# Queries, keys and values of a four-layer graph network from seven block products

## The chip, the cores and the metric

The kernel runs on one core of a Trainium2 chip. The metric is device time in microseconds of one execution. The five engines of the core work side by side: TensorE (PE, with its weight loads shown as PEld), VectorE (DVE), ScalarE (ACT), GpSimd (POOL) and SyncE (SP), which issues the DMA transfers. They wait for one another only through semaphores.

## The reference

128 graphs of 64 nodes with 256 features pass through four layers; before each, the features are normalised and clipped at zero, and each layer's result is added to them.

```python
# layers 0 and 1: attention with 8 heads of 32, masked by (or biased with the log of) the adjacency
q, k, v = h @ Wq, h @ Wk, h @ Wv                 # layer 0 with biases
attn = softmax(q @ k.T / sqrt(32) + mask)        # per head, over the 64 nodes of a graph
x = x + (attn @ v) @ Wo + bo
# layer 2: five steps of a gated unit over the graph
m = h @ weight[l]; agg = A.T @ m; h = gru(agg, h)
# layer 3: a gate between two products
x = x + elu(gate * (adj @ (h @ theta) * norm) * norm + (1 - gate) * (h @ W_h))
```

Everything is float32. The kernel takes 8 graphs at a time as a group: 512 tokens, four pairs of 128. There are 16 groups, and a group has two halves of 256 tokens.

## The kernel before

The kernel doesn't issue its instructions in the order in which they are written. Each operation is put into a plan with the engine, an assumed cost in ns, what it reads and writes, and a place in a strand; at the end the plan plays the five engines against each other, picks the next operation by its key among those that are ready, and so fixes the order of instructions on every engine. Parts of three groups are interleaved in this way: the attention of one, the gated unit of the one before, layer 3 of the one before that.

```python
def mm(n, count=1):                       # assumed cost of a float32 product of n columns
    return count * 2 * (n / 1.2 + 2.5)
INTO, OUT, BESIDE, ALONE = 110, 260, 0.3, 0.1   # into and out of small tiles; preferences in the choice
...
if found:                                 # in Plan.run: the choice of the next operation
    first = min(at for at, _ in found) + 15
    alone = ALONE if sum(t[1].small and t[0] <= first + 100 for t in found) < 2 else 0.0
    pick = min((t for t in found if t[0] <= first), key=lambda t: t[1].key + (
        (-BESIDE if small else alone) if t[1].small else 0.0))
```

The attention of one half. Weights of q, k, v stay in SBUF; `hT` holds the normalised features, transposed, in two chunks of 128 features.

```python
def attend(layer, xt, half, bias, bias_at, name):
    ...
    def dense(ps, wt, dst):
        for c in range(2):
            for kc in range(2):
                pe(mm(256), lambda c=c, kc=kc: nc.tensor.matmul(
                    ps[:, c * HALF : (c + 1) * HALF], wt[:, kc, c * P : (c + 1) * P], hT[:, kc, :],
                    start=kc == 0, stop=kc == 1), [wt, hT], [ps], holds=[dst])

    pq = bank(f"q_{name}")                       # one of 4 PSUM banks with tag "a"
    dense(pq, w["q"], qT)
    ...                                          # VectorE: q out of PSUM (+ bias in layer 0) into qT
    pk = bank(f"k_{name}")
    dense(pk, w["k"], k_exp)
    ...                                          # ScalarE: k out of PSUM, spread over two masked copies
    if waiting:
        ...
        def both():
            weigh_last()                         # of the half before: attn @ v, 32 products in 64x32 tiles
            scores()                             # of this half: q @ k.T, 16 products in 64x64 tiles
        pe(1440, both, [*reads, qT, k_exp], [*po_last, *pss], holds=[oT_last, *es], small=True)
        finish_last()
    else:
        pe(870, scores, [qT, k_exp], pss, holds=es, small=True)
    pv = bank(f"v_{name}")
    for gp in range(2):
        for kc in range(2):
            pe(mm(256), ...)                     # v
    sca(act(512), ...)                           # ScalarE: v out of PSUM
    ...                                          # softmax on DVE, ACT and POOL; four transposes
```

Elsewhere the kernel already forms 2x2 block products with seven in place of eight: in the gated unit (256 columns) and in layer 3 (384 columns), where two banks take turns and each product adds to what an earlier one left:

```python
def seven_products(hT, F, name):                 # layer 3
    T = new("hTT", [P, 4, P], 1, f"hTT_{name}")
    ...                                          # VectorE: 4 differences of blocks of hT
    product(1, pb, True)
    product(2, pc, True)
    total(pc, keep(pb, "l1"), 0, 0)              # keep: ScalarE evicts; total: VectorE adds
    product(5, pc, True)
    p5 = keep(pc, "l5")
    product(6, pb)
    u = keep(pb, "lu")
    product(3, pc)
    total(pc, u, 0, 1)
    product(7, pb)
    total(pb, p5, 1, 1)
    product(4, pb)
    ...
F = [new("F", [P, 3, D], 3, f"F_{g}_{2 * half + i}") for i in range(2)]      # 3 buffers
```

Of the kernel before, what the change touches and what calls it, by code (L numbers as in the profile page):

```python
# [46 lines left out]
INTO, OUT, BESIDE, ALONE = 110, 260, 0.3, 0.1  # L47
AHEAD = 1.7
# [4 lines left out]
FRONT_LAST = 0.1  # L53
FRONT_SPAN = 1.1
BACK = -0.1
BACK_LAST = 0.6
BACK_SPAN = 0.6
STEP = -0.2
# [8 lines left out]
FUSE = -1.05  # L67
# [3 lines left out]
def mm(n, count=1):  # L71
    return count * 2 * (n / 1.2 + 2.5)
# [45 lines left out]
class Op:  # L118
    __slots__ = ("eng", "cost", "lat", "fn", "key", "left", "users", "ready", "vals", "port", "small")


class Plan:
# [15 lines left out]
    def add(self, eng, cost, fn, reads=(), writes=(), lat=None, early=0.0, holds=(), port=False, small=False):  # L138

        op = Op()  # L140
        op.eng, op.cost, op.fn, op.users, op.ready = eng, cost, fn, [], 0.0
        op.lat = AFTER[eng] if lat is None else lat
        op.port, op.small = port, small
        op.key = self.at - early
        if eng == "PE":
            self.at += cost
        deps, vals = set(), []
        items = [(False, r) for r in reads] + [(True, w) for w in writes]
        items = [(wr, it if isinstance(it, tuple) else (it, None)) for wr, it in items]
        for wr, (v, part) in items:  # L150
            if v not in vals:
                vals.append(v)
            for table in (v.writers, v.readers) if wr else (v.writers,):
                for k, ops in table.items():
                    if part is None or k is None or k == part:
                        deps.update(ops)
        for wr, (v, part) in items:
            if wr:
                if part is None:
                    v.writers, v.readers = {}, {}  # L160
                v.writers[part], v.readers[part] = [op], []
            else:
                v.readers.setdefault(part, []).append(op)
        for v in holds:
            vals.append(v)
            for ops in v.readers.values():
                deps.update(ops)
        deps.discard(op)
        op.left = len(deps)
        for d in deps:  # L170
            d.users.append(op)
        op.vals = vals
        for v in vals:
            if not v.left and v.slots.queue is not None:
                v.slots.queue.append(v)
            v.left += 1
        self.ops.append(op)
# [6 lines left out]

    def run(self):
# [5 lines left out]
        ready, small = {e: [] for e in AFTER}, False  # L191
# [6 lines left out]
        for _ in range(len(self.ops)):  # L198
# [3 lines left out]
            for eng, ops in ready.items():  # L202
# [16 lines left out]
                if found:  # L219
                    first = min(at for at, _ in found) + 15  # L220
                    alone = ALONE if sum(t[1].small and t[0] <= first + 100 for t in found) < 2 else 0.0
                    pick = min((t for t in found if t[0] <= first), key=lambda t: t[1].key + (
                        (-BESIDE if small else alone) if t[1].small else 0.0))
                    if best is None or pick[0] < best[0]:
                        best = pick
# [9 lines left out]
            if op.eng == "PE":  # L235
                end += (INTO if op.small else OUT) if op.small != small else 0
                small = op.small
# [17 lines left out]
def gnn_stack_kernel(ctx: ExitStack, tc: tile.TileContext, a: dict, out: bass.AP):  # L255
# [18 lines left out]
    def new(tag, shape, n, name=None):  # L274
        if tag not in tags:
            home = psum if tag in ("a", "g") else dram if tag == "gates" else work
            tags[tag] = Slots(home, tag, n, tag in ("g", "ht", "agg", "Ta", "Th", "gv", "qT", "kexp", "v"))
# [8 lines left out]
    def pe(cost, fn, reads, writes, early=0.0, holds=(), small=False):  # L286
        plan.add("PE", cost, fn, reads, writes, early=early, holds=holds, small=small)
# [65 lines left out]
    with plan.strand(-3.0, 0.1):  # L353
# [31 lines left out]
        attn = [[{n: load_w(f"L0_gnn_W{n}", D) for n in "qk"}]]  # L385
# [11 lines left out]
        attn[0][0]["v"] = load_w("L0_gnn_Wv", D)  # L397
# [6 lines left out]
        attn[0][0]["o"] = load_w("L0_gnn_Wo", D)  # L404
        attn[0].append(load_row("L0_gnn_bo"))
# [3 lines left out]
        attn.append([{n: load_w(f"L1_gnn_W{n}", D) for n in "qkvo"}, load_row("L1_gnn_bo")])  # L409
# [22 lines left out]
    with plan.strand(-0.9, 0.1):  # L432

        w, bo = attn[0]
        bvb = new("aT", [P, 4, P], 2, "bvb")
        pbo = bank("bvo")
        for c in range(2):
            vec(200, lambda c=c: nc.vector.tensor_copy(
                bvb[:, c, :], cols[:, 16 + c : 17 + c].to_broadcast([P, P])), [cols], [(bvb, c)])
            pe(mm(256), lambda c=c, w=w: nc.tensor.matmul(  # L440
                pbo[:, :D], bvb[:, c, :], w["o"][:, c, :], start=c == 0, stop=c == 1),
                [(bvb, c), w["o"]], [pbo])
# [34 lines left out]
    def transposed(dst, dst_at, src, src_at, name, on_act, writes, relu=False, early=0.0,  # L477
# [12 lines left out]
        pe(437, turn, [*(reads or [src]), ident], [ps], early, [dst])  # L490
# [37 lines left out]


    waiting = []  # L530

    def attend(layer, xt, half, bias, bias_at, name):

        w, bo = attn[layer]
        biased = layer == 0
        pp = 2 * half
        hT = normed(xt, half, name, True)
        k_exp = new("kexp", [P, 2, 2, HALF], 1, f"kexp_{name}")
        qT = new("qT", [P, 2, HALF], 1, f"qT_{name}")

        def dense(ps, wt, dst):
            for c in range(2):
                for kc in range(2):
                    pe(mm(256), lambda c=c, kc=kc: nc.tensor.matmul(  # L544
                        ps[:, c * HALF : (c + 1) * HALF], wt[:, kc, c * P : (c + 1) * P], hT[:, kc, :],
                        start=kc == 0, stop=kc == 1), [wt, hT], [ps], holds=[dst])

        pq = bank(f"q_{name}")
        dense(pq, w["q"], qT)
        if biased:  # L550
            for c in range(2):
                vec(dve(256, 1), lambda c=c: nc.vector.tensor_scalar(
                    qT[:, c, :], pq[:, c * HALF : (c + 1) * HALF], cols[:, c : c + 1], None, op0=ALU.add),
                    [pq, cols], [(qT, c)])
        else:
            vec(dve(512), lambda: nc.vector.tensor_copy(
                qT.tile, pq.tile.rearrange("p (c t) -> p c t", c=2)), [pq], [qT])
        v = new("v", [P, 2, D], 2, f"v_{name}")
        pk = bank(f"k_{name}")
        dense(pk, w["k"], k_exp)  # L560

        for par in range(2):
            if biased:
                for c in range(2):
                    sca(act(256, 2), lambda c=c, par=par: nc.scalar.activation(
                        k_exp[:, c, par, :], pk[:, c * HALF : (c + 1) * HALF], AF.Identity,
                        bias=few[:, k_bias + 2 * c + par : k_bias + 2 * c + par + 1],
                        scale=few[:, parity + par : parity + par + 1]),
                        [pk, (few, 2), (few, 3 + c)], [(k_exp, (par, c))])
            else:  # L570
                sca(act(512, 1), lambda par=par: nc.scalar.activation(
                    k_exp[:, :, par, :], pk.tile.rearrange("p (c t) -> p c t", c=2), AF.Copy,
                    scale=few[:, parity + par : parity + par + 1]), [pk, (few, 2)], [(k_exp, (par, 0)), (k_exp, (par, 1))])
# [3 lines left out]
        def scores():  # L577
            for i in range(2):
                for c in range(2):
                    for gp in range(2):  # L580
                        for rh in range(2):
# [4 lines left out]
                                             qT[s, c, t0 : t0 + NODES], k_exp[s, c, :, t0 : t0 + NODES],  # L586
# [3 lines left out]
        if waiting:  # L590
            _, weigh_last, reads, po_last, oT_last, finish_last = waiting.pop()

            def both():
                weigh_last()
                scores()

            pe(1440, both, [*reads, qT, k_exp], [*po_last, *pss], holds=[oT_last, *es], small=True)
            finish_last()
        else:
            pe(870, scores, [qT, k_exp], pss, holds=es, small=True)  # L600

        pv = bank(f"v_{name}")
        for gp in range(2):
            for kc in range(2):
                pe(mm(256), lambda gp=gp, kc=kc: nc.tensor.matmul(  # L605
                    pv[:, gp * D : (gp + 1) * D], hT[:, kc, gp * P : (gp + 1) * P],
                    w["v"][:, kc, :], start=kc == 0, stop=kc == 1),
                    [w["v"], hT], [pv], holds=[v])
        sca(act(512), lambda: nc.scalar.activation(
            v.tile, pv.tile.rearrange("p (g f) -> p g f", g=2), AF.Copy), [pv], [v])  # L610
# [6 lines left out]
        for i in range(2):  # L617
# [25 lines left out]
            pe(437, turn, [e, ident], [pa], holds=[aT])  # L643
# [21 lines left out]
        def finish():  # L665
# [4 lines left out]
            for i in range(2):  # L670
                for c in range(2):
                    pe(mm(256), lambda i=i, c=c: nc.tensor.matmul(  # L672
                        py[:, i * D : (i + 1) * D], oT[:, i, c, :], w["o"][:, c, :],
                        start=c == 0, stop=c == 1), [(oT, i), w["o"]], [py])
# [6 lines left out]
    def flush(xt):  # L681
# [4 lines left out]
        pe(470, weigh, reads, po, holds=[oT], small=True)  # L686
# [16 lines left out]
    def fuse_weights(l):  # L703
# [11 lines left out]
        pe(437, turn, [gw[l], ident], [ps], holds=[wT, gv])  # L715
# [27 lines left out]
    def gru(h, ht, A, name):  # L743
# [19 lines left out]
        for l in range(LAYERS):  # L763
# [65 lines left out]
            pe(930, total, [ht, A], banks, holds=[agg], small=True)  # L829
# [120 lines left out]
    def front(g):  # L950
# [10 lines left out]
        for layer in range(2):  # L961
# [3 lines left out]
            for half in range(2):  # L965
# [3 lines left out]
                attend(layer, xt, half, bias, bias_at, f"{g}_{layer}_{half}")  # L969
# [23 lines left out]
        pe(437, turn, [blk, ident], [ps], holds=[adjT])  # L993
# [85 lines left out]
    def back_half(g, xt, h, adjT, norm, half):  # L1079
# [9 lines left out]
        pe(437, turn, [(h, (0, half)), (h, (1, half)), ident], [ps])  # L1089
# [8 lines left out]
        F = [new("F", [P, 3, D], 3, f"F_{g}_{2 * half + i}") for i in range(2)]  # L1098
# [40 lines left out]
    with plan.strand(FIRST, FIRST_SPAN):  # L1139
        for g in ORDER:  # L1140
            next(parts[g])
        for _ in parts[0]:
            pass
    for l in range(LAYERS):
# [68 lines left out]
```

## Time and profile before

| | |
|---|---|
| time, median of 3 runs | 2570.04 us (2569.54 to 2570.05) |
| span in the profile | 2566.7 us |
| granted TensorE clock | 0.998 |
| DMA traffic | 145.54 MB, mean 57 GB/s |
| q and k products | x512 instructions each, 386 and 382 ns mean |
| v products | x512 instructions, 381 ns mean |
| scores (s), weighing (o) | x2048 and x4096 instructions |
| aggregation (agg) | x5120 instructions |
| exp of the scores (ACT) | x128, 629 ns |

How to read it: a page gives for each engine its busy time; a group of instructions is named by the line of the kernel, the engine, the operation and what it writes and reads ("q<-hT,w_L_gnn_Wq"). The mean duration of one matmul is longer than the time it takes up in a stream, since matmuls overlap; the distance between the starts of two in a row is what a stream pays. "128*128" is the part of the array that a matmul uses, "128x256" its moving operand. Each float32 product stands in the trace as two weight loads and two matmuls.

### The profile page before, as it was taken

The numbers are of one execution on the slowest core, as the hardware profiler recorded it, in microseconds if no ns is written. First come the engines' busy times: TensorE is split into PE (matmuls) and PEld (weight loads), VectorE is DVE, ScalarE is ACT, GpSimd is POOL, SyncE is SP. The second block draws the span as 40 slices with busy tenths as digits, with TensorE's granted clock in tenths as the row PEclk, the third lists the DMA queues.
The fourth block names the chain that finished last, engine by engine and source line by source line (L and its number), as shares of the span: only waits on it lengthen the run. The fifth ranks groups of instructions, "written<-read, shape, count | busy, mean of one in ns | idle before, by whom it ended". The sixth has DMA issues, their size and how long they took to land.

```text
span 2566.7 us, 54470 instructions
## 1 busy us (share of the span) xinstructions
PE 2534.6 (99%) x22445; PEld 2129.0 (83%) x22445; DVE 1947.9 (76%) x4137; ACT 1308.8 (51%) x2452; POOL 870.4 (34%) x890
## 2 busy tenths in 40 slices
PE   8999999999999999999999999999999999999997
PEld 6788888888888888888888888888888888888885
DVE  6776677877777787787877878777777877777767
ACT  4445555555545555555554555555455455545543
POOL 5533332423233242432423324232332424323221
PEclk9999999999999999999999999999999999999999
DMA  5311111111111111211111111111111112011110
GB/s 156 119 64 56 58 44 61 44 48 61 49 57 44 48 61 48 76 35 59 43 67 57 44 65 44 48 57 48 57 44 48 57 48 77 24 48 70 61 57 17
DMA packets 44203, 145.54 MB, mean 57 GB/s; under 512 B 11106, under 2 KB 32820, under 8 KB 33076
## 3 DMA queue, kind: packets, MB, share of 16 engines
q1 hardware_dynamic: 43840, 142.03, 15.7%
q8 instruction: 177, 2.90, 0.5%
q14 instruction: 70, 0.57, 0.1%
q10 hardware_dynamic: 116, 0.04, 0.0%
HBM read 126.79 MB, written 15.27 MB: 55 GB/s over the span
## 4 chain that ended last, share of the span: by engine, by line
PE 96%; DVE 3%; ACT 0%; DMA 0%; issue 0%; POOL 0%; SPq 0%; DVEq 0%; POOLq 0%
PE gb L785 22%; PE gc L785 16%; PE nb L785 11%; PE nc L785 8%; PE q L544 4%; PE v L605 4%; PE k L544 4%; PE y L672 4%; PE agg L825 3%; PE l3b L1050 3%; PE s L585 3%; PE aT L640 2%; PE l3c L1050 2%; PE hT L488 2%; PE lnT L488 2%; PE o L659 2%
## 5 line engine op out<-in xcount | busy, mean ns | idle before, releaser
L894 POOL TENSOR_TENSOR sn<-h,sn 128x512 f32<-128x512 f32 x160 | 211.3, 1321 | 652.1 <-ACT sn L892 652.1
L634 POOL TENSOR_TENSOR e<-e,ssum 128x512 f32<-128x512 f32 x128 | 145.6, 1149 | 338.7 <-DVE ssum L633 324.3
L785 PE MATMUL gb<-Ta,gv 128*128 128x256 f32 x960 | 249.2, 382 | 0.0
L785 PE MATMUL gb<-Th,w_hh 128*128 128x256 f32 x960 | 248.2, 381 | 0.0
L474 POOL TENSOR_TENSOR rstd<-pw,few 128x2 f32<-128x2 f32 x128 | 119.6, 937 | 313.7 <-DVE pw L473 307.3
L892 ACT ACTIVATE sn<-sn,b_n 128x512 f32<-128x512 f32 x160 | 116.0, 725 | 172.8 <-DVE sn L890 172.0
L785 PEld LDWEIGHTS gb<-Th,w_hh 128*128 128x128 f32 x960 | 179.7, 190 | 27.5 <-issue 2.7
L785 PEld LDWEIGHTS gb<-Ta,gv 128*128 128x128 f32 x960 | 177.0, 190 | 28.7 <-issue 4.1
L754 POOL TENSOR_TENSOR Th<-h 128x256 f32<-128x256 f32 x160 | 118.4, 760 | 226.9 <-PE nb L785 173.5
L785 PE MATMUL gc<-h,w_hh 128*128 128x256 f32 x640 | 166.9, 383 | 0.6 <-ACT sg L884 0.5
L888 DVE SCALAR_TENSOR_TENSOR sn<-sg,sn 128x512 f32<-128x512 f32 x160 | 120.2, 751 | 58.5 <-ACT sn L942 55.6
L785 PE MATMUL gc<-agg,gv 128*128 128x256 f32 x640 | 164.3, 379 | 0.0
L630 ACT ACTIVATE e<-e 128x512 f32<-128x512 f32 x128 | 80.0, 629 | 163.2 <-DVE e L628 161.9
L877 ACT ACTIVATE sg<-sg,b_rz 128x512 f32<-128x512 f32 x160 | 108.1, 716 | 99.0 <-DVE sg L857 99.0
L838 DVE TENSOR_TENSOR Ta<-agg 128x256 f32<-128x256 f32 x160 | 82.8, 557 | 99.0 <-ACT sg L884 36.2
L544 PE MATMUL q<-hT,w_L_gnn_Wq 128*128 128x256 f32 x512 | 148.8, 386 | 1.5 <-DVE e L621 0.8
L544 PE MATMUL k<-hT,w_L_gnn_Wk 128*128 128x256 f32 x512 | 148.9, 382 | 0.0
L785 PE MATMUL nb<-Th,w_hh 128*128 128x256 f32 x480 | 144.4, 382 | 0.0
L785 PE MATMUL nb<-Ta,gv 128*128 128x256 f32 x480 | 143.0, 379 | 0.0
L785 PEld LDWEIGHTS gc<-agg,gv 128*128 128x128 f32 x640 | 121.4, 190 | 19.4
L896 DVE SCALAR_TENSOR_TENSOR sn<-sg,sn 128x512 f32<-128x512 f32 x160 | 112.5, 703 | 31.8 <-POOL sn L894 31.6
L785 PEld LDWEIGHTS gc<-h,w_hh 128*128 128x128 f32 x640 | 118.8, 190 | 19.6 <-issue 2.4
(164 smaller groups left out, 6472.4 us busy)
## 6 DMA issues: line engine op xcount, KB each, us to landing
gv<-gates SPq DMA_DIRECT2D x80, 1344.0 KB, 5.8
x<-in_x_dram SPq DMA_DIRECT2D x32, 256.0 KB, 5.6
out_dram<-x SPq DMA_DIRECT2D x32, 256.0 KB, 2.2
gates<-gv SPq DMA_DIRECT2D x5, 1344.0 KB, 5.1
adjq<-in_adj_dram SPq DMA_DIRECT2D x8, 256.0 KB, 3.0
gw<-in_L_gnn_weight_dram SPq DMA_DIRECT2D x5, 256.0 KB, 5.8
w_ih<-in_L_gnn_w_ih_dram SPq DMA_DIRECT2D x2, 384.0 KB, 5.4
w_hh<-in_L_gnn_w_hh_dram SPq DMA_DIRECT2D x2, 384.0 KB
```

What stands on the lines that cost most here:

```text
L474: pool(680 if n == 2 else 1220, lambda: nc.gpsimd.tensor_tensor(dst.tile, s.tile, few[:, 1 : 1 + n], op=ALU.pow), [s, (few, 1)], [dst])
L488: nc.tensor.transpose(to, src_at(i), ident.tile)
L544: pe(mm(256), lambda c=c, kc=kc: nc.tensor.matmul(ps[:, c * HALF : (c + 1) * HALF], wt[:, kc, c * P : (c + 1) * P], hT[:, kc, :], start=kc ...
L634: pool(1000, lambda e8=e8, z=z: nc.gpsimd.tensor_tensor(e8(), e8(), z[:, :, None].to_broadcast(shape), op=ALU.mult), [e, z], [e])
L754: pool(690, lambda: nc.gpsimd.tensor_tensor(T[:, i, :], x(), y(), op=ALU.subtract), reads, [(T, i)])
L785: nc.tensor.matmul(bank_[:, col * HALF : (col + 1) * HALF], at(g, n), rhs(), start=first and j == 0, stop=True, skip_group_check=True)
L877: sca(act(TOK, 1.5), lambda k=k, col=col: nc.scalar.activation(g_v[:, :, k, :], g_v[:, :, k, :], AF.Tanh, bias=b_rz[:, col : col + 1], sca ...
L888: vec2(dve(TOK), lambda: nc.vector.scalar_tensor_tensor(a_(), r(), 1.0, a_(), op0=ALU.add, op1=ALU.mult), [*ts[0], n_v], [n_v])
L892: sca(act(TOK, 1.5), lambda: nc.scalar.activation(a_(), a_(), AF.Tanh, bias=b_n[:, oc : oc + 1]), [n_v, b_n], [n_v])
L894: pool(1230, lambda: nc.gpsimd.tensor_tensor(b_(), hh(), a_(), op=ALU.subtract), [*hp, n_v], [n_v])
L896: vec2(dve(TOK, 1), lambda: nc.vector.scalar_tensor_tensor(b_(), z(), 1.0, b_(), op0=ALU.add, op1=ALU.mult), [*ts[1], n_v], [n_v])
L1050: pe(mm(384), lambda: nc.tensor.matmul(bk[:, : 3 * P], b(), w3[:, :, n, :], start=first, stop=True, skip_group_check=True), [w3, *reads], ...
```

## The change

The q, k and v weights of a layer are seen as 2x2 blocks of 128x128 (output block by input block), and so is the transposed input (feature chunk by token pair). With the seven-product scheme, q, k and v of a half come from seven sets of three products of 128 columns, in place of twelve products of 256 columns. Four of the seven sets of weights are sums or differences of blocks. They are formed once for each layer, all seven are stored in DRAM, and they are loaded again for each group and layer into seven SBUF buffers, which both halves of the group use. The first uses (layer 0 of groups 0 and 1, layer 1 of group 0) keep the plain products.

```diff
+    def weights_of(xt, layer, half, name):
+        if (xt, layer) not in taken_in:
+            blocks = taken_in[xt, layer] = {}
+            for i in (1, 2, 5, 6, 3, 7, 4):
+                t = blocks[i] = new("qw", [P, 3, P], 7, f"qw{i}_{name}")
+                dma(192, lambda i=i, t=t: nc.sync.dma_start(t.tile, kept[layer, i].tile), [kept[layer, i]], [t])
+        return taken_in[xt, layer] if not half else taken_in.pop((xt, layer))
...
+        def by_seven():
+            T = new("hTQ", [P, 4, P], 1, f"hTQ_{name}")
+            ...                                  # VectorE: 4 differences of 128 columns
+                def go():
+                    for j in range(3):
+                        lhs, rhs = (w[:, j, :], b()) if j < 2 else (b(), w[:, j, :])
+                        nc.tensor.matmul(bk[:, j * P : (j + 1) * P], lhs, rhs,
+                                         start=first and j == 0, stop=True, skip_group_check=True)
+                pe(3 * mm(128), go, [w, *reads], [bk], holds=[qk, v])
...
+            def keep(bk, nm, c):
+                ...                              # ScalarE: 384 columns (128 + 256 with a bias in layer 0)
+            def total(bk, t, c, gp):
+                vec(dve(256), ...)               # q and k
+                vec(dve(128), ...)               # v
+            product(1, pb, True)
+            product(2, pc, True)
+            total(pc, keep(pb, "q1", 0), 0, 0)
+            product(5, pc, True)
+            p5 = keep(pc, "q5", 1)
+            product(6, pb)
+            u = keep(pb, "qu", 0)
+            product(3, pc)
+            total(pc, u, 0, 1)
+            product(7, pb)
+            total(pb, p5, 1, 1)
+            product(4, pb)
+            ...                                  # ScalarE: the last block out of PSUM
+            spread(lambda c: qk[:, c, :, 1, :], [qk])    # k spread by ScalarE, now from SBUF
```

The weighing of the half before and the scores of this one become two operations of the plan, and the plan knows four modes of TensorE and what each change between them costs:

```diff
-            def both():
-                weigh_last()
-                scores()
-
-            pe(1440, both, [*reads, qT, k_exp], [*po_last, *pss], holds=[oT_last, *es], small=True)
+            pe(655, weigh_last, reads, po_last, holds=[oT_last], mode=T32)
+            pe(860, scores, [qk, k_exp], pss, holds=es, mode=T64)
...
-INTO, OUT, BESIDE, ALONE = 110, 260, 0.3, 0.1
-AHEAD = 1.7
+WIDE, T64, T32, TURN = range(4)
+CHANGE = ((0, 95, 95, 0), (250, 30, 135, 200), (237, 135, 30, 187), (0, 95, 95, 0))
+BESIDE = 0.2
+ALONE = 0.1
+TURNING = 0.05
+AHEAD = 1.75
...
 def mm(n, count=1):
-    return count * 2 * (n / 1.2 + 2.5)
+    return count * 2 * max(n / 1.2 + 2.5, 112)
```

To make room in SBUF, layer 3's tile `F` goes from three buffers to two, and q, k, v weights borrow buffers of the gated unit's state at the start. Some constants that place the strands of the plan are set anew (`FRONT_LAST` 0.1 to 0.15, `FRONT_SPAN` 1.1 to 0.9, `BACK_LAST` 0.6 to 0.85, `STEP` -0.2 to 0.0, `FUSE` -1.05 to -1.1).

## The prediction

> **What bounds the kernel now.** I read the page's shares first, then the chain that ended last, then the list of what TensorE waited for, and last the timeline of the repeating middle. The first two, from the page:
>
> ```profile
> span 2566.7 us, 54470 instructions
> PE 2534.6 (99%) x22445; PEld 2129.0 (83%) x22445; DVE 1947.9 (76%) x4137; ACT 1308.8 (51%) x2452; POOL 870.4 (34%) x890
> PE 96%; DVE 3%; ACT 0%; DMA 0%; issue 0%; POOL 0%; SPq 0%; DVEq 0%; POOLq 0%
> ```
>
> TensorE is never without work and is 96% of the chain. "Busy" alone would not prove that it runs at its pace, so I looked at its waits. The three longest of the whole execution are
>
> ```profile
> PE pc L423 <- DMA w_L_gnn_Wv<-in_L_gnn_Wv_dram: 8.5, 1, 8.5
> PE l3b L1050 <- DVE hTT L1039: 5.0, 2, 4.6
> PE lnT L488 <- DVE xn L514: 3.6, 3, 2.0
> ```
>
> The first is the start, before any work; all the others together sum to 15 us, over 2567. The middle is an unbroken stream. Stretches of one group each (columns: stretch, length, then busy time of PE, PEld, DVE, ACT, POOL, clock, DMA share, GB/s) show it:
>
> ```profile
> 1114.09:1269.84 155.75, 155.75 (x1397) 131.63 (x1397) 121.36 (x259) 82.75 (x154) 53.38 (x53) 1.00 0.16 54
> 1269.84:1425.60 155.76, 155.76 (x1398) 131.63 (x1397) 122.33 (x259) 79.68 (x151) 53.41 (x53) 1.00 0.15 52
> ```
>
> One group costs 155.76 us, PE fills all of it, and DVE fills 122 us (78%). So in the middle only TensorE's own work counts, and what is taken off it counts in full as long as the other engines keep up.
>
> **What one instruction costs in place.** A float32 product is two matmul instructions here (q: 64 halves x 4 products, x512 instructions). Their mean duration is not their cost, because they overlap; the distance between starts is. From the timeline of the matmuls (start, length of the piece, what, count):
>
> ```profile
> 1000.71 1.03 PE L785 MATMUL gc<-agg,gv 128*128 128x256 f32 x4
> 1002.00 0.60 PE L640 MATMUL aT<-ident,e 128*128 128x128 f32 x4
> 1014.55 1.03 PE L785 MATMUL gb<-h,w_hh 128*128 128x256 f32 x4
> 1015.51 0.86 PE L659 MATMUL o<-aT,v 64*32 64x64 f32 x64
> 1016.30 1.10 PE L585 MATMUL s<-kexp,qT 64*64 64x128 f32 x32
> 1017.33 1.13 PE L785 MATMUL gb<-Ta,gv 128*128 128x256 f32 x4
> ```
>
> Four with 256 moving columns start over (1.03 - 0.38)/3 = 0.216 us each (0.38 is the duration of one). Four transposes with 128 columns start every (0.60 - 0.27)/3 = 0.109 us. The new products have 128 columns but load ordinary float32 weights, which no transpose does (its load takes 0.141 us, theirs 0.190). Would the load hold them at more than 0.109? The timeline of the weight loads answers:
>
> ```profile
> 1002.33 0.30 PEld L544 LDWEIGHTS k<-hT,w_L_gnn_Wk 128*128 128x128 f32 x2
> ```
>
> Two ordinary loads of 0.190 us fit in 0.30 us, so the second began 0.110 after the first: behind 128-column matmuls, ordinary loads do follow each other at 0.110. In all of the trace's records some 580 pairs of full-array loads start 0.108 to 0.110 apart and none closer. That is the number on which the prediction stands.
>
> **What the Trainium skill says.** "TensorE: Matmul & The Clock Gate", section "LDWEIGHTS (loading the stationary operand)": the load costs its columns divided by 1.2 per ns, so 107 ns for 128; the trace agrees (0.108 to 0.110 between starts, with a duration of 0.190 that includes a latency). The same page, "Back-to-back issue gap": with 128 columns a stream of load and matmul pairs is paced by both, 81 ns where the matmul alone would take 56. This is not for float32, and this trace has no stream of 128-column float32 products, so it is my main doubt. "TensorEngine Tiling (Array Packing)", "Key Properties": changing the tiling mode drains TensorE. The trace agrees: from the last full-array start before the o and s products (1014.55 + 3 x 0.216 = 1015.20) to the next at 1017.33 is 2.13 us, and the four there take 0.10 us longer than the usual 1.03; less one ordinary step of 0.216 the episode costs 2.02 us. "Perfetto Trace Analysis", "Identifying the Most-Contended Engine": matmul busy time is a poor measure, look at weight loads. These are at 83%, which is why the pace of the load had to be settled.
>
> **The change part by part.**
>
> *Products.* Before, a half (256 tokens of a group, one layer) has 12 products of 256 columns for q, k and v: 24 x 0.216 = 5.18 us. After, 7 x 3 = 21 products of 128 columns: 42 x 0.110 = 4.62 us. As 42 short instructions in seven sets, each behind a wait, will not all be at the floor, I take the 0.112 which the change's plan also assumes: 4.70 us. Saved: 0.48 us a half (0.56 at the floor). Layer 0 of groups 0 and 1 and layer 1 of group 0 stay plain, 6 of the 64 halves; 58 x 0.48 = 28 us, or 32 at the floor. I use **-29 us**. A full group should fall from 155.76 by about 2.0 us. Note how thin this is: 42 short instructions replace 24 long ones, so each 0.002 us on a step takes 0.08 us off a half's gain, and at 5.18 / 42 = 0.123 all of it is gone.
>
> *VectorE.* Added per half: four subtractions of 128 columns (layer 3 has the same: 465 ns twice in a mean of 430, then 284), about 1.4 us; three pairs of sums, 256 and 128 columns, which I estimate from layer 3's 384 columns at 550 ns as 0.42 + 0.28, so 2.1 us. Removed: the copy of q, 0.94 us (two of 470) in layer 0, 0.69 in layer 1. Net 2.6 to 2.8 us, 11 a group: 122 becomes 133 of some 154 us, 86% (less where durations overlap). High, but below TensorE.
>
> *ScalarE.* Added: three evictions (490 ns of 384 columns; two instructions with a bias in layer 0) and the last product's, two or three short ones; removed: v's 594 ns. I estimate 1.5 to 2.9 us a half, 9 a group, 81 to 90 of 154. The copies that spread k stay, now from SBUF.
>
> *Weights by DMA.* 29 group-layers x 7 blocks x 192 KB is 40 MB beside 145.5 MB. A block is loaded again once the second half has used it; each half takes about a quarter of a group, near 39 us, while the present 1344 KB of gate weights land in 5.8 us. DMA share rises from 0.16 to about 0.2. Hidden.
>
> *Scores and weighing apart.* Before, all but one pair of these ran as one, 62 times at 2.02 us; the 80 aggregations always stood alone, 1.29 us by the same reckoning (1.40 between starts). Always apart, weighing would cost 0.99 (seen once) and scores about 1.2 (an estimate: 2.02 less 0.99, plus the drain in and out that they now pay): +0.17 x 62 = +11 us. If one in every pair found an aggregation beside it, it would save about 0.2 to 0.3 us each, -15 us at best. Both become eligible at nearly the same place in the plan, so I expect most to stay paired: **-2 us**.
>
> *Start and end.* The setup sums and stores 14 blocks, beside other work. Layer 3's tile goes from three buffers to two; in the last group, whose halves had little else to run, that may cost a few us. With the busier VectorE and two of four PSUM banks held through seven dependent products, I add **+6 us** of waits over the whole.
>
> Sum: 2570 - 29 - 2 + 6 = 2545.
>
> **The rivals.**
> 1. *The load sets the pace.* If 128-column float32 products run at 0.123 or more because load and matmul don't overlap fully, the gain is nil: 2570 to 2590. For it: loads are busy 83% and last 0.190. Against: 0.110 between ordinary loads, seen hundreds of times.
> 2. *VectorE or the seven-step chain becomes the bound.* TensorE would show repeated idle before the new products, and groups would stay near 155 us: 2560 to 2580. For it: TensorE's longest wait after the start is in just such a chain, that of layer 3. Against: those are 5.0 us in 30 chains, and 4.6 of them are one wait at 2534 us, where little else was left to run.
> 3. *The freer plan gives more than the products.* Aggregations, weighing and scores side by side, drains saved: 2520 to 2530. For it: 142 separate episodes now. Against: the plan before also favoured neighbours and had none.
>
> **Range and chances.** Products give -32 to -22, switches -15 to +11, waits 0 to +15. Combined, 8 in 10 lie in 2526 to 2563. Faster by over 2% (below 2518.6) needs the best of both first terms: 0.05. Slower by over 2% needs a new bound: 0.02.
>
> **What would show it.** A group of 153.5 to 154.0 us, PE full; the new products 0.109 to 0.113 between starts; DVE near 85% with no new line among TensorE's waits; episodes of weighing and scores still mostly in pairs. Starts at 0.12 and above, or waits of several us on the new sums in every group, would make it wrong.

## The result and the profile after

The changed kernel takes 2581.2 us (2580.99 to 2581.93, 4 runs) against 2569.91 before, a ratio of 1.0045 (95% interval 1.0027 to 1.0062): slower by 11 us, where 25 us of gain were forecast, and outside the range. The page after, its span, its shares and its chain:

```profile
span 2579.5 us, 58085 instructions
PE 2526.5 (98%) x23489; PEld 2144.7 (83%) x23489; DVE 2086.3 (81%) x4647; ACT 1401.4 (54%) x2796; POOL 856.8 (33%) x890
PE 87%; DVE 9%; ACT 2%; issue 1%; POOL 1%; DMA 0%; ACTq 0%; POOLq 0%; DVEq 0%
```

TensorE is busy for 8 us less than before, in a span that is 13 us longer, and the chain has handed 9 points of its 96% to the other engines. Two groups of the middle (columns as in the prediction: stretch, length, PE, PEld, DVE, ACT, POOL, clock, DMA share, GB/s):

```profile
1122.00:1278.62 156.62, 155.01 (x1470) 132.52 (x1469) 132.51 (x294) 89.32 (x178) 52.33 (x53) 1.00 0.21 71
1278.62:1435.24 156.62, 154.99 (x1470) 132.40 (x1469) 132.49 (x294) 86.25 (x175) 52.37 (x53) 1.00 0.21 70
```

A group takes 156.62 us in place of 155.76, and for 1.6 us of it TensorE does nothing, where before it never stopped. What it waits for now (us in total, times, longest), the start left out:

```profile
PE aT L773 <- POOL e L767: 9.7, 15, 2.1
...
PE l3c L1183 <- DVE F L1195: 6.1, 11, 0.6
...
PE qkvc L669 <- DVE v L690: 2.8, 12, 0.2
PE gc L918 <- DVE sg L990: 2.4, 12, 0.4
```

Four waits that come back in almost every group (11 to 15 times), on VectorE and GpSimd, and none on the new weights. The new products themselves run at the pace that was assumed. The timeline of the matmuls:

```profile
1125.44 0.61 PE L669 MATMUL qkvb<-hT,qw 128*128 128x128 f32 x4
1125.88 0.39 PE L669 MATMUL qkvb<-qw,hT 128*128 128x128 f32 x2
```

Its first line holds four starts 0.113 us apart ((0.61 - 0.27)/3, where 0.27 is the duration of one); over all steps within these products the median is 0.112.

I went through all starts of matmuls, from the first to the last, and split each distance into the step that the instruction needs in a stream (0.109 us at 128 columns), the extra time around episodes of small tiles, and the rest, which is waiting and slower steps. The split is good to about 2 us, and is used for all kernels below:

| us | before | after |
|---|---|---|
| full-array products and transposes | 2283.3 | 2248.8 |
| products in small tiles | 173.9 | 173.9 |
| changes of tiling | 59.4 (145 episodes) | 64.3 (169 episodes) |
| the rest | 34.0 | 75.3 |

The products gave 34.5 us back, or about 27 with the 2436 new instructions at their 0.112. The changes of tiling took 4.9, the rest 41.3, of which 7 are these slower steps and 34 are waits. (The idle time that the profile shows for TensorE grows by 21 us only: a matmul that still runs covers part of a wait, and the step after a wait is slow, by 0.10 us in the group above.) In one group of the middle the rest is 0.5 us before and 3.7 us after. The question is what the 34 us wait for.

**One collision, followed.** The timeline of one group of the changed kernel, VectorE and GpSimd:

```profile
1127.89 0.28 DVE L1172 TENSOR_TENSOR hTT<-hT,hTT 128x128 f32<-128x128 f32 x1
...
1128.09 1.45 DVE L535 TENSOR_SCALAR xn<-x,mv,rstd 128x256 f32<-128x256 f32 x1
1128.13 1.26 POOL L1027 TENSOR_TENSOR sn<-h,sn 128x512 f32<-128x512 f32 x1 [2.08 <-ACT sn L1025]
...
1129.47 0.28 DVE L1172 TENSOR_TENSOR hTT<-hT,hTT 128x128 f32<-128x128 f32 x1
```

The normalisation `xn` usually takes 0.41 us. Here it takes 1.45, because GpSimd's subtraction `sn` began just as VectorE passed from one operation to the next. All that follows on VectorE without a gap is 1.04 us late, and one of those operations is the sum that TensorE's next layer-3 product needs:

```profile
1130.80 0.55 DVE L1195 TENSOR_TENSOR F<-l3c,l 128x384 f32<-128x384 f32 x1
...
1131.40 0.91 PE L1183 MATMUL l3c<-w,hTT 128*128 128x384 f32 x2 [0.55 <-DVE F L1195]
```

TensorE stands for 0.55 us, in 11 groups at the same place. `xn` neither reads nor writes what `sn` does, so no semaphore makes it wait: the statement ahead of the prediction that the engines wait for one another only through semaphores does not hold for these two. The Trainium skill describes the cause on the page "SBUF — State Buffer", section "Who interferes with whom": VectorE's second pair of SBUF ports is GpSimd's only pair, and it is locked, not shared. The trace agrees as far as it can (1.45 us for 0.41; by the records `xn` even started 0.04 us before `sn`, and was held all the same), and shows what the plan had not reckoned with. The plan knows the lock (`locked`), but gives it to GpSimd only after VectorE has left it alone for 60 ns. Here VectorE's operations follow each other without such a pause, and GpSimd got in all the same.

The longest of the four waits in total comes about in the same way, and there one of the new differences is held:

```profile
1244.52 1.31 POOL L767 TENSOR_TENSOR e<-e,ssum 128x512 f32<-128x512 f32 x1 [6.30 <-DVE ssum L766]
1244.85 1.13 DVE L653 TENSOR_TENSOR hTQ<-hT 128x128 f32<-128x128 f32 x1
...
1247.15 1.51 POOL L767 TENSOR_TENSOR e<-e,ssum 128x512 f32<-128x512 f32 x1 [1.33 <-DVE ssum L766]
...
1248.72 0.66 PE L773 MATMUL aT<-ident,e 128*128 128x128 f32 x4 [0.56 <-POOL e L767]
```

The difference `hTQ` usually takes 0.29 us. Held by GpSimd for 0.84, it makes VectorE's next `ssum` late, GpSimd's next `e` waits for that, and TensorE for `e`. In this group each of the four waits has an operation of VectorE that was held within 5 us before it; 21 are held by over 0.3 us in the group, and three of them stand before the four waits.

### The profile page after: what moved, and what is told of

The parts are those of the page before. It is cut to its first block, busy times and chain, and to the rows that moved or that the text cites. A ratio compares the mean times of both kernels' runs of the same rounds, so it can differ in the third digit from the quotient of the medians.

```text
span 2579.5 us, 58085 instructions
## 1 busy us (share of the span) xinstructions
PE 2526.5 (98%) x23489; PEld 2144.7 (83%) x23489; DVE 2086.3 (81%) x4647; ACT 1401.4 (54%) x2796; POOL 856.8 (33%) x890
## 4 chain that ended last, share of the span: by engine, by line
PE 87%; DVE 9%; ACT 2%; issue 1%; POOL 1%; DMA 0%; ACTq 0%; POOLq 0%; DVEq 0%
PE gb L918 19%; PE gc L918 15%; PE nb L918 10%; PE nc L918 7%; PE qkvb L669 5%; PE y L805 4%; PE qkvc L669 4%; PE agg L958 3%; PE s L731 3%; PE l3b L1183 2%; PE hT L509 2%; PE l3c L1183 2%; PE lnT L509 2%; PE o L792 2%; PE aT L773 2%
## 5 line engine op out<-in xcount | busy, mean ns | idle before, releaser
L495 POOL TENSOR_TENSOR rstd<-pw,few 128x2 f32<-128x2 f32 x128 | 104.7, 819 | 357.3 <-DVE pw L494 351.4
L918 PEld LDWEIGHTS gb<-Th,w_hh 128*128 128x128 f32 x960 | 174.3, 190 | 26.2 <-issue 0.8
L535 DVE TENSOR_SCALAR xn<-x,mv,rstd 128x256 f32<-128x256 f32 x256 | 125.4, 525 | 31.1 <-POOL rstd L495 15.6
L1029 DVE SCALAR_TENSOR_TENSOR sn<-sg,sn 128x512 f32<-128x512 f32 x160 | 109.5, 684 | 50.6 <-POOL sn L1027 50.5
L1021 DVE SCALAR_TENSOR_TENSOR sn<-sg,sn 128x512 f32<-128x512 f32 x160 | 135.8, 849 | 12.3 <-ACT sn L1075 7.8
L887 POOL TENSOR_TENSOR Th<-h,Th 128x256 f32<-128x256 f32 x160 | 138.1, 863 | 11.5 <-DVE h L1031 5.8
L805 PE MATMUL y<-w_L_gnn_Wo,oT 128*128 128x256 f32 x512 | 135.1, 383 | 0.5 <-DVE oT L800 0.5
L1031 DVE SCALAR_TENSOR_TENSOR h<-sn 128x512 f32<-128x512 f32 x160 | 128.4, 802 | 2.8
L1023 DVE SCALAR_TENSOR_TENSOR sn<-sn 128x512 f32<-128x512 f32 x160 | 128.4, 802 | 0.9
```

The source lines that it names most:

```text
L535: vec2(325, lambda p=p, i=i: nc.vector.tensor_scalar(xn[:, i, :], xt[:, p, :], mv[:, i, 0:1], rstd[:, i : i + 1], op0=ALU.subtract, op1=AL ...
L805: pe(mm(256), lambda i=i, c=c: nc.tensor.matmul(py[:, i * D : (i + 1) * D], oT[:, i, c, :], w_o[:, c, :], start=c == 0, stop=c == 1), [(oT ...
L887: pool(690, lambda: nc.gpsimd.tensor_tensor(T[:, i, :], x(), y(), op=ALU.subtract), reads, [(T, i)])
L918: nc.tensor.matmul(bank_[:, col * HALF : (col + 1) * HALF], at(g, n), rhs(), start=first and j == 0, stop=True, skip_group_check=True)
L1021: vec2(dve(TOK), lambda: nc.vector.scalar_tensor_tensor(a_(), r(), 1.0, a_(), op0=ALU.add, op1=ALU.mult), [*ts[0], n_v], [n_v])
L1023: vec2(dve(TOK), lambda: nc.vector.scalar_tensor_tensor(a_(), a_(), 0.5, b_(), op0=ALU.mult, op1=ALU.add), [n_v], [n_v])
```

## The experiments

Theory A: the change fills VectorE, GpSimd takes the port between operations which the plan meant to follow each other, and TensorE, whose order is fixed, waits. Theory B: VectorE simply has too much work. Theory C: the new order is bad for reasons of its own, the freer plan included.

**Narrower GpSimd operations, same order.** Two of GpSimd's operations work on 32 of 512 columns; the rest is left out. Every engine's order is unchanged.

```diff
-nc.gpsimd.tensor_tensor(b_(), hh(), a_(), op=ALU.subtract)
+nc.gpsimd.tensor_tensor(b_()[:, :, :16], hh()[:, :, :16], a_()[:, :, :16], op=ALU.subtract)
-nc.gpsimd.tensor_tensor(e8(), e8(), z[:, :, None].to_broadcast(shape), op=ALU.mult)
+nc.gpsimd.tensor_tensor(e8()[:, :, :4], e8()[:, :, :4], z[:, :, None].to_broadcast([P, HEADS, 4]), op=ALU.mult)
```

> The changed kernel in the same order on every engine, but two of GpSimd's operations work on a part of their columns only: the subtraction of the gated unit on 32 of 512 columns, the normalisation of the scores on 32 of 512 (the rest is left out, so the output is not the reference's). They fall from 1.3 and 1.1 us to some 0.4. Theory A (VectorE operations that read and write SBUF stand still while GpSimd works, and TensorE, whose order is fixed, waits for them): the waits of about 3 us a group fall to under 1, a group from 156.6 to about 154, the whole from 2581 to 2540 to 2550. Theory B (VectorE simply has too much work of its own): its work is the same, so at most 10 us are gained. Theory C (the new order is bad in itself, for its chains on TensorE, ScalarE and PSUM banks): no change, 2575 to 2585.

> The control: the kernel before with the same two operations narrowed, in its own unchanged order. Theory A: it waits only some 0.5 us a group for such things, so it gains 0 to 15 us, 2555 to 2570, clearly less than the changed kernel does. If it gains as much as the changed kernel (30 us and more), the narrowing does something else than to remove what the change brought, and theory A is not supported.

Measured: the changed kernel falls to 2541.9 us (2540.33 to 2542.99), by 39; the kernel before to 2563.9, by 5.5. The rest falls from 75.3 to 36.6 us. The stretch of one group:

```profile
1108.00:1261.60 153.60, 153.60 (x1470) 132.78 (x1469) 126.30 (x294) 88.88 (x179) 35.59 (x53) 1.00 0.22 73
```

TensorE is full again (the rest of a group is 0.7 us), with the same VectorE instructions in the same order. That speaks against B and C. It leaves one rival: shorter GpSimd operations also shorten the chains that run through GpSimd.

**GpSimd made to wait, same order.** To rule that out, nothing is made shorter and GpSimd alone is delayed: each of its operations waits for the VectorE operation that the plan had put ahead of it at the port. The kernel is complete.

```diff
+def behind(self, op, made, ahead):
+    if op.port and op.eng == "DVE":
+        return made
+    if op.port and ahead is not None:
+        self.tc.add_manual_dep(made.ins, ahead.ins.name, ...)      # made starts after ahead has ended
+    return ahead
```

> The changed kernel, complete, in its own order on every engine; the one addition is that each GpSimd operation that uses the shared port waits for the VectorE operation which the plan had put ahead of it at the port (95 more waits of GpSimd on VectorE in the program). Nothing becomes shorter; GpSimd alone starts later. Theory A (GpSimd gets in between two operations of VectorE which the plan had meant to follow each other, and VectorE then stands still for a microsecond): the stream goes as planned, TensorE's waits fall from 3 us a group to about 1, the whole 2540 to 2560, though GpSimd has been delayed. If the narrowed operations only helped because the chain through GpSimd became shorter, this run must be slower than the changed kernel: 2581 to 2610.

> The control to the last: the kernel before, in its own order, with GpSimd waiting in the same way for the VectorE operation that its plan had put ahead of it. Theory A: the order before has few such collisions that reach TensorE (0.5 us of waits a group), so it gains little, 2555 to 2570, against the 32 us that the changed kernel gained. If it gains 20 us and more, the collisions were there before and are not what the change brought.

Measured: 2549.0 us (2548.05 to 2550.17), 32 us less than the changed kernel, and 0.9920 (0.9904 to 0.9937) of the kernel before; the kernel before gains 2 us at most from the same (2566.9, ratio 0.9992, 0.9983 to 1.0001). The same place in its timeline:

```profile
1116.34 0.28 DVE L1172 TENSOR_TENSOR hTT<-hT,hTT 128x128 f32<-128x128 f32 x1
...
1116.54 0.41 DVE L535 TENSOR_SCALAR xn<-x,mv,rstd 128x256 f32<-128x256 f32 x1
...
1116.86 0.28 DVE L1172 TENSOR_TENSOR hTT<-hT,hTT 128x128 f32<-128x128 f32 x1
...
1118.09 1.27 POOL L1027 TENSOR_TENSOR sn<-h,sn 128x512 f32<-128x512 f32 x1
```

`xn` is back at 0.41 us, and GpSimd's subtraction starts 1.55 us behind it where it had started on top of it. A group takes 153.9 us, of which the rest is 1.0 us; over the whole the rest is 43.2 us, 32 less than in the changed kernel. An engine was delayed and the kernel became faster: theory A is shown, and the explanation by shorter chains falls.

**Less VectorE work, same order.** The four differences of input blocks are made in 8 of 128 columns, and the products read one column of them spread out; the rest is left out.

```diff
-nc.vector.tensor_tensor(T[:, n, :], x(), y(), op=ALU.subtract)
+nc.vector.tensor_tensor(T[:, n, :8], x()[:, :8], y()[:, :8], op=ALU.subtract)     # y: T for n = 1, 3
-b, reads = (lambda: T[:, t, :]), [(T, t)]
+b, reads = (lambda: T[:, t, :1].to_broadcast([P, P])), [(T, t)]
```

> The changed kernel in its own order, with the four differences of the input's blocks made on VectorE in 8 of 128 columns only (464 of 696 operations that the change adds to VectorE in the middle of the kernel; the products read one column of them spread out, so the output is not the reference's). GpSimd's operations stay as they are. Each falls from some 0.20 us of VectorE's time to some 0.08, in all 464 x 0.12 = 56 us of VectorE. Theory A (who gets the shared port decides): the operations still have to wait for the port, most collisions stay, 2565 to 2580. Theory B (the amount of VectorE's work decides): this takes away about two fifths of the work that the change added, so some 15 us of the 30 to 35 us of waits go, 2560 to 2568; more than that would speak for it strongly.

The count in it is twice too high: there are 58 x 4 = 232 such operations, so the work taken away is some 29 us (287 ns to 160 at the median), and theory B should have given back about 8 us (15 x 29 / 56). Measured: 2578.5 us (2577.32 to 2578.79), 3 us less; a group 156.38. Amount counts for something, but an operation of 8 columns can be held as well (the longest took 1.00 us). This run alone tells A and B apart only weakly.

**The plan's rule for the port.** The plan is told that GpSimd, if ready, goes ahead when VectorE's operation ends.

```diff
-if best is None or pick[0] < best[0]:
+if best is None or pick[0] < best[0] or (eng == 'POOL' and pick[0] <= best[0]):
...
-locked[op.eng] = end + 60
+locked[op.eng] = end                            # changed kernel
+locked[op.eng] = end + (-60 if op.eng == 'DVE' else -200)     # kernel before
```

> The changed kernel with one thing altered in the plan's reckoning: a GpSimd operation that is ready takes the shared port as soon as VectorE's running operation ends, ahead of VectorE's next, in place of 60 ns after a pause of VectorE. All computation is the same, the order of instructions comes out new. Theory A: an order that was made with the right expectation of who gets the port has fewer waits of TensorE: 2535 to 2560. Theories B and C: the order is only another one, 2570 to 2600.

> The kernel before with the same correction in its plan (the port given to GpSimd 60 ns before VectorE's operation ends by the plan, and back to VectorE 200 ns before GpSimd's ends). It has little to gain, as its middle shows 0.5 us of waits a group: 2550 to 2572 by theory A. If it falls by 20 us or more, then the correction is worth more than the seven products, and the kernel before was held by the port too.

Measured: the changed kernel 2554.8 us (2551.56 to 2555.92), ratio 0.9943 (0.9928 to 0.9958), all computation in place; 153.84 a group in the middle, but 139.9 from the first aggregation to that of the next group, where the kernel before takes 131.4. The kernel before becomes slower, 2578.6, which was not expected: its old order had hardly any such waits to lose (rest 34.0), the new one has more (43.4). The two corrections differ in their numbers, so this pair is no clean comparison.

**Both kinds of products under one rule.** The second form of the rule (`end`) for all, and for each kernel some placing constants set anew (7 in the first, 14 in the second, 6 in the third; the first's and third's are shown).

```diff
 # seven_apart: the whole change
-BESIDE, AHEAD, BACK_LAST, BACK_END, ENTRY, FUSE, FUSE_SPAN = 0.2, 1.75, 0.85, -0.05, 0.05, -1.1, 0.45
+BESIDE, AHEAD, BACK_LAST, BACK_END, ENTRY, FUSE, FUSE_SPAN = 0.45, 1.6, 0.2, -0.1, 0.25, -1.2, 0.25
 # seven_joined: weighing and scores one operation again
-pe(655, weigh_last, reads, po_last, holds=[oT_last], mode=T32)
-pe(860, scores, [qk, k_exp], pss, holds=es, mode=T64)
+pe(1650, both, [*reads, qk, k_exp], [*po_last, *pss], holds=[oT_last, *es], mode=T32, leaves=T64)
 # plain_joined: the kernel before
-AHEAD, BACK_LAST, BACK_SPAN, STEP_LAST, LOCK, FIRST_SPAN = 1.7, 0.6, 0.6, -0.1, 0.3, 1.1
+AHEAD, BACK_LAST, BACK_SPAN, STEP_LAST, LOCK, FIRST_SPAN = 1.75, 0.05, 0.65, -0.3, 0.35, 0.9
```

(The expectation of the first says eight; seven are set.)

> The whole change with the corrected rule for the port, and its placing constants set anew under that rule (eight of them). The corrected kernel with the change's own constants took 2554.8: 153.85 a group in the middle, but 8.5 us more than the kernel before in its first group and 1.3 in its second. Theory A expects the middle to stay near 153.7 and some of the start to come back: 2538 to 2555. If the middle goes back over 155, the gain of the corrected rule was chance.

> The same with weighing and scores as one operation of the plan again (its constants set anew as well). The changed kernel had 169 episodes of small tiles where the kernel before had 145, and paid 4.9 us more for the changes of tiling. If the split costs what its episodes cost and the order gains nothing from it: 3 to 6 us less than with the split, 2535 to 2550. If the freedom is worth more than the drains: 3 us or more above it.

> The kernel before (plain products, weighing and scores as one) with the corrected rule for the port, and six of its constants set anew under it. Theory A: it has little to gain in the middle, where its order already waits only 0.5 us a group: 2550 to 2575, and the seven products under the same rule are faster by 10 to 30 us. If it comes out as fast as the seven products, the rule was all, and the products are worth nothing.

| | us | ratio to before | group | changes of tiling | the rest |
|---|---|---|---|---|---|
| seven products, apart | 2541.9 | 0.9893 (0.9878 to 0.9908) | 153.94 | 64.8 | 36.9 |
| seven products, joined | 2549.4 | 0.9922 (0.9907 to 0.9937) | 153.88 | 59.9 | 46.5 |
| plain products, joined | 2570.0 | 1.0003 (0.9994 to 1.0011) | 155.64 | 59.1 | 36.5 |

Groups alternate a little; the figure is the mean of two. With a plan that knows how the port is given out, the seven products are worth 20.6 us (2570.0 to 2549.4), 1.76 a group, though each kernel has constants of its own. Split or joined makes no difference in the middle (153.94, 153.88): the split's 4.9 us of drains stand in the table, and the joined version gives more than that away in waits (the rest is 46.5 in place of 36.9), some 3 us of it in the first 155 us, 2 us near the end, and the remainder in small parts, with constants of its own. What the freer plan is worth by itself stays open. The first version beats both kernels; its page and one of its groups:

```profile
PE 2508.9 (99%) x23489; PEld 2144.6 (84%) x23489; DVE 1979.6 (78%) x4647; ACT 1405.0 (55%) x2796; POOL 832.1 (33%) x890
1110.00:1263.95 153.95, 153.95 (x1469) 132.62 (x1468) 123.57 (x293) 89.60 (x178) 50.32 (x53) 1.00 0.22 73
```

VectorE has the same 4647 instructions as in the changed kernel and is "busy" for 107 us less (1979.6, 2086.3). Nearly all of that was operations that stood still: the profile counts a held operation as busy, and the time by which operations were held falls from 183 to 54 us (last section).

## Why the prediction was wrong

- *What bounds the kernel, and the pace of the new products*: right. TensorE's steps set the time before, each of the two instructions of a 128-column float32 product takes 0.112 us, and the pair of ordinary loads 0.110 apart had told it in advance. The main doubt (rival 1, the weight load) did not come true. (The 580 pairs of loads, none closer, leave out the loads for transposes, some of which start 0.056 us apart.)
- *The saving of the products*, 29 us: right, about 27 at the measured step.
- *VectorE's load*: the estimate was 133 us a group, and 132.5 were measured. That they agree is luck: part of the 132.5 is standing still. Under one rule for the port it is 116.5 us with plain products and 123.5 with seven (both joined), so the added work is 7 us and not 11. ScalarE's 90 came out as 86 to 89. There was room on VectorE; "high, but below TensorE" looked at the amount alone.
- *Waits over the whole, +6 us*: this is the step that failed. They came to 34. I asked whether VectorE had room, not when it may use the port and who else wants it. The change puts 232 more operations that use the shared port into a schedule in which GpSimd's own come at fixed places, under a rule that has GpSimd wait for a pause, and it makes the whole order anew. In the order before GpSimd got in as well, but few of its collisions reached TensorE (0.5 us a group). That the collisions cost the time is shown; whether the added operations or the new order brought them stays open: of 273 operations held, 56 are the new differences, and of the three that stand before TensorE's waits in the group above one is.
- *Scores and weighing apart, -2 us*: +4.9 by the changes of tiling. Pairs did not stay together: of 64, 25 did; 38 scores and 26 weighings stood alone, and 14 episodes joined an aggregation. The sign was wrong, the size small.
- *Sum*: 2545 + 28 (waits, 34 in place of 6) + 7 (tiling) + 2 (products) = 2582, and 2581.2 was measured.
- *Rival 2* named VectorE and the seven-step chain, with 2560 to 2580. The direction was right, the mechanism was not: with the same VectorE instructions the kernel runs at 2541.9 or 2549.0 us.
- *A sign was in the profile before.* Layer 3's differences, which I took as the model of the new ones, had a mean of 465 ns for one half of them and 283 ns for the other, at the same shape; the median of the first half is 287. I took this for the cost of the instruction. It was the mark of operations that are held: 22 of these 60 took over 0.3 us longer, each while GpSimd worked.

## What to carry to other kernels

Ask of a new VectorE operation not only how long it takes but whether it reads and writes SBUF alone while GpSimd works, and look at the spread of such rows: a mean far above the median, at an unchanged shape, was here the mark of waiting for the port, which no idle column shows. Where the order of instructions is fixed in advance, one microsecond of it can come back as a wait of the bounding engine in every round (here 0.55 us in 11 groups), so the rule by which the schedule gives out the port can be worth as much as the saving that it schedules (here 32 us beside 27). An engine off the critical path may have to be delayed on purpose.

## What the runs showed of the hardware

GpSimd gets the shared port between two VectorE operations that follow each other at once: at 1128.09 us `xn` was held 1.04 us by an operation that had become ready only then. In the changed kernel 273 of VectorE's 4647 operations take over 0.3 us longer than the median of the same operation and shape, 183 us in all (before: 174, 110 us). Each of the 273 overlaps an operation of GpSimd in time, and each reads and writes SBUF alone. With GpSimd made to wait it is 185 and 113 us, in the fastest version 84 and 54 us: what held operations cost here depended on who waited for them, not on their number alone.
